# A Mamba block with a routed expert layer: steps of a round respread over two PSUM banks, activations bound in the ScalarE order, transfers taken out of a branch

## The chip, the cores and the metric

The kernel runs on one core of a Trainium2 chip. The metric is the device time of one execution in microseconds (us), as the median of several runs. The profile comes from one further execution, which has a time of its own.

## The reference

The input is a sequence of T = 4096 tokens of width D = 256, in float32. Cut to what matters:

```python
xz = x @ W_in                                   # 256 -> 2 * 512
y = depthwise_conv(xz[:, :512], conv_w, 4 taps, causal) + conv_b
convolved = silu(y)
x_dbl = convolved @ W_x                         # delta (1), B (16), C (16)
delta = softplus(x_dbl[:, :1])
h[t] = exp(delta[t] * A) * h[t-1] + delta[t] * B[t] * convolved[t, :16]
ssm_out[t] = sum(h[t] * C[t])                   # one number per token
out = ((ssm_out + convolved * D_param) * silu(xz[:, 512:])) @ W_out
x = layernorm(x + out)
expert = argmax(x @ Wr.T + br)                  # one of 8 experts per token
x = layernorm(x + W2[expert] @ relu(W1[expert] @ x + b1[expert]) + b2[expert])
```

Each expert has W1 of 1024 x 256 and W2 of 256 x 1024. Only the chosen expert of a token is computed in the kernel.

## The kernel before

**First half, by rounds.** The tokens are cut into NB = 8 tiles of TB = 512. The loop over `k` (L752) is a software pipeline. Round k projects tile k in eight steps `project(k, 0..7)` (two matmuls of 128x512 each, into a PSUM tile `pm`), and between these steps it does pieces of older tiles: of tile a = k-1 `gauge` (delta, B and C, PSUM tiles `px` and `pxo`), `look_out` (the router's raw scores, `pf`) and `scan` (`pt`); of tile b = k-2 `gate` (`py`), four `project_out` (`po`) and `choose` (the expert of each token); of tile c = k-3 `rank` (a token's place in its expert's list, `pr`), `blocks_of` (a table of blocks, `pn`), `place` (writes the lists, `pz`) and `tokens_of` (looks a block's tokens up, `pi`).

**Second half, by blocks.** A block is 128 tokens of one expert; there are at most NSB = 39, and `SURE` = 37 is the number that is always worked off outside the branch. A block has four quarters: `hidden(b, 0)`, `hidden(b, 1)` (PSUM `ph`, 16 matmul records each), `close(b, 0)`, `close(b, 1)` (PSUM `pe`). `close(b, 1)` adds the token and the bias, does the layer norm and writes the 128 rows to `out` with an indirect DMA ("the scatter", L432). `turn(b)` transposes the gathered tokens (`pg`, then a VectorE copy to `xgT`). `expert(n)` takes the next n quarters; a table `fill` says how many go between the steps of rounds 6 and 7, and after the rounds a written-out list mixes the last steps with `expert` calls. The rest of the quarters then runs alone: this stretch is called the plain tail below.

**What sets the order.** TensorE's (PE's) order is the program's order (L100). On the other engines a scheduler orders the instructions; they then run in that order, each waiting on semaphores. PSUM has eight banks: three under the tag `mm` (`pm`, `ph`), three under `o` (`py`, `po`, `pe`) and two under `tr`, which `px`, `pxo`, `pr`, `pn`, `pf`, `prx`, `pz`, `pt`, `pi` and `pg` take in turn. So each user of `tr` waits until the second last one before it has been read out.

**Transfers of the blocks.** `prefetch(b)` issues, on GpSimd's (POOL's) queue, the gather of a block's tokens (`xg`, four buffers) and of its expert's 2.2 MB of weights (`we`, three buffers), up to `AHEAD` = 2 blocks ahead and here not beyond block 36. A scatter to `out` waits for the scatter before it to land, since both write `out`.

**The branch.** When the table of the last tile is built, every engine loads the number of tokens, `total`, into a register (L267). After block 34 comes the branch for blocks 37 and 38; it holds their gathers, their weights and their scatters. Blocks 35 and 36 come behind it:

```python
    quarters = blocks(0, SURE - 2)
...
    with tc.If(held[0] > (SURE - EARLY[6]) * P, preferred_fallthrough_block=False):
        for _ in blocks(SURE, NSB):
            pass
    for _ in blocks(SURE - 2, SURE):
        pass
```

With these inputs the branch is not taken.

Of the kernel before, what the change touches and what calls it, by code (L numbers as in the profile page):

```python
# [33 lines left out]
F32 = mybir.dt.float32  # L34
# [3 lines left out]
AF = mybir.ActivationFunctionType  # L38
# [5 lines left out]
P = 128  # L44
# [3 lines left out]
TB = 512  # L48
# [31 lines left out]
def mamba_moe(  # L80
# [158 lines left out]
    def table(b0, nb, columns, rows, early):  # L239
# [110 lines left out]
        nc.scalar.copy(wout[:, :, D : D + NE], pov)  # L350


    xgs, wes, turned, hid, last, open_ = {}, {}, {}, {}, {}, {}
    current = 0

    def prefetch(b):
        for n in range(b, min(b + AHEAD, SURE - 1) + 1) if b < SURE else (b,):
            if n in index and n not in xgs:
                xgs[n] = m3.tile([P, D], F32, tag="xg", name=f"xg{n}", bufs=4)
                nc.gpsimd.indirect_dma_start(  # L360
                    out=xgs[n], out_offset=None, in_=x1d[0 : index[n][0], :],
                    in_offset=bass.IndirectOffsetOnAxis(ap=index[n][1], axis=0),
                )
            if n in weights and n not in wes:

                wes[n] = (
                    wes[SURE] if n > SURE else m3.tile([P, WROW], F32, tag="we", name=f"we{n}")
                )
                nc.gpsimd.indirect_dma_start(  # L369
                    out=wes[n][:, :], out_offset=None, in_=experts,  # L370
                    in_offset=bass.IndirectOffsetOnAxis(ap=weights[n], axis=0),
                )

    def turn(b):

        px = bank("tr", f"pg{b}", 2)
        for dc in range(DC):
            nc.tensor.transpose(
                px[:, dc * P : (dc + 1) * P], xgs[b][:, dc * P : (dc + 1) * P], ident
            )  # L380
        turned[b] = (
            turned[SURE] if b > SURE else m2.tile([P, DC * P], F32, tag="xgT", name=f"xgT{b}")
        )
        nc.vector.tensor_copy(turned[b], px[:, 0 : DC * P])

    def hidden(b, half):
# [23 lines left out]
    def close(b, half):  # L410
        xg, we = xgs[b], wes[b]
        hT = hid[b]
        if half == 0:
            open_[b] = bank("o", f"pe{b}")
        py = open_[b]
        for fc in range(half * FC // 2, (half + 1) * FC // 2):
            at = O2 + fc * D
            nc.tensor.matmul(  # L418
                py[:, 0:D], lhsT=hT[:, fc, :], rhs=we[:, at : at + D],
                start=(fc == 0), stop=(fc == FC - 1),  # L420
            )
# [10 lines left out]
        nc.gpsimd.indirect_dma_start(  # L432
            out=out, out_offset=bass.IndirectOffsetOnAxis(ap=index[b][1], axis=0),
            in_=y[:, 0, :], in_offset=None, bounds_check=T - 1, oob_is_err=False,
        )

    def blocks(*span):

        nonlocal current
        for b in range(*span):  # L440
            current = b
            prefetch(b)
            if b not in turned:
                turn(b)
            hidden(b, 0)
            yield
            hidden(b, 1)
            yield
            if b + 1 in xgs:
                turn(b + 1)  # L450
            close(b, 0)
            yield
            close(b, 1)
            yield

    quarters = blocks(0, SURE - 2)

    def expert(n=1):
        for _ in range(n):
            next(quarters)  # L460
# [3 lines left out]
    def project(i, c):  # L464

        s = st[i]
        xTb = s["xTb"]
        if c == 0:
            s["xc"] = a2.tile([P, CC, KC - 1 + TB], F32, tag="xc", name=f"xc{i}")
            s["cv"] = a3.tile([P, CC, TB], F32, tag="cv", name=f"cv{i}")  # L470
            s["sg"] = a3.tile([P, CC, TB], F32, tag="sg", name=f"sg{i}")
            if i == 0:
                nc.gpsimd.memset(s["xc"][:, :, 0 : KC - 1], 0.0)
            else:
                nc.gpsimd.tensor_copy(
                    s["xc"][:, :, 0 : KC - 1], st[i - 1]["xc"][:, :, TB : TB + KC - 1]
                )
        xc, cv, sg = s["xc"], s["cv"], s["sg"]
        pm = bank("mm", f"pm{i}_{c}")
        for dc in range(DC):  # L480
            nc.tensor.matmul(  # L481
                pm, lhsT=win[:, dc, c * P : (c + 1) * P], rhs=xTb[:, dc, :],
                start=(dc == 0), stop=(dc == DC - 1),
            )
        if c >= CC:
            nc.scalar.activation(sg[:, c - CC, :], pm, AF.Silu)  # L486
            return
        nc.scalar.copy(xc[:, c, KC - 1 :], pm)  # L488
        acc = a3.tile([P, TB], F32, tag="acc", name=f"acc{i}_{c}")
        nc.scalar.activation(  # L490
            acc, pm, AF.Identity, scale=cw[:, c, KC - 1 : KC], bias=cb[:, c : c + 1]
        )
        for k in range(KC - 1):
            nc.vector.scalar_tensor_tensor(  # L494
                acc, xc[:, c, k : k + TB], cw[:, c, k : k + 1], acc, ALU.mult, ALU.add
            )
        nc.scalar.activation(cv[:, c, :], acc, AF.Silu)  # L497

    def gauge(i):

# [305 lines left out]
    expert(2)  # L806
    gauge_out(a)
    expert()
    rank(c)
    blocks_of(c)  # L810
    expert(2)
    project_out(b, 0)
    expert()
    look_out(a)
    project_out(b, 1)
    scan(a)
    expert()
    project_out(b, 2)
    expert()
    place(c)  # L820
    project_out(b, 3)
    choose(b)
    expert(2)
    tokens_of(c)
    gate(a)
    expert(3)
    rank(b)
    expert(2)
    project_out(a, 0)
    expert()  # L830
    project_out(a, 1)
    expert()
    project_out(a, 2)
    place(b)
    project_out(a, 3)
    choose(a)
    expert(4)
    rank(a)
    blocks_of(a)
    expert(5)  # L840
    place(a)
    expert(2)
    tokens_of(a)
    for _ in quarters:
        pass

    with tc.If(held[0] > (SURE - EARLY[6]) * P, preferred_fallthrough_block=False):
        for _ in blocks(SURE, NSB):
            pass
    for _ in blocks(SURE - 2, SURE):  # L850
        pass


# [42 lines left out]
```

## Time and profile before

| | |
|---|---|
| median of 3 runs | 561.43 us (560.48 to 561.77) |
| the profiled execution, its own time | 563.69 us |
| its span in the profile | 562.0 us |
| PE busy | 508.3 us (90%) |
| VectorE (DVE) busy | 344.7 us (61%) |
| ScalarE (ACT) busy | 223.8 us (40%) |
| POOL busy | 174.7 us (31%) |
| DMA queue of POOL (gathers, weights, scatters) | 91.65 MB, 43.8% of 16 engines' span |
| weights of a block, issue to landing | 9.7 us (median of 37) |

Busy time is the time in which an engine has an instruction in work. Idle time before an instruction is put down to the event that came last before it, its releaser; `DVE oh L667` is a VectorE instruction of line 667 that writes `oh`. "PEclk" is the TensorE clock that was granted, as a share of the full one. The 1.69 us between the span and the execution's own time lie outside the span.

### The profile page before, as it was taken

What the parts mean: (1) busy time and instruction counts of PE and PEld (TensorE: products, weight loads), DVE (VectorE), ACT (ScalarE), POOL (GpSimd) and SP (SyncE); (2) the same over time, 40 slices, a digit from 0 to 9 for tenths busy, and PEclk for the clock granted to TensorE, in tenths of its full rate; (3) what the DMA queues carried; (4) which work ended last, traced back from release to release, by engine and by line L of the source; (5) the groups of instructions that cost most, each with busy time, mean ns of one, the idle gap of its engine ahead of it and who ended that gap; (6) DMA issues with size and microseconds to landing.
All of it is one profiled execution on the core that took longest, in us unless ns stands there. A gap on an engine that the chain in (4) does not pass through costs nothing. (4 is left out here: it accounts for less than half of the span.)

```text
span 562.0 us, 7926 instructions
## 1 busy us (share of the span) xinstructions
PE 508.3 (90%) x2780; PEld 385.7 (69%) x2780; DVE 344.7 (61%) x1156; ACT 223.8 (40%) x461; POOL 174.7 (31%) x191
## 2 busy tenths in 40 slices
PE   5898999898889499999789998999999999999890
PEld 2353545455354377577578787999999999999790
DVE  0656969496976684995748868545555444445531
ACT  0858768475746365564733202111111111111110
POOL 2001221233353241442333322334433343444210
PEclk9989999899979699999979999999999999999997
DMA  8201012120319404604646556989989999999800
GB/s 239 83 23 38 0 38 75 35 79 1 114 43 428 156 10 169 227 17 170 219 147 260 206 200 213 342 316 341 346 329 348 336 345 340 336 346 349 326 21 0
DMA packets 23018, 106.94 MB, mean 190 GB/s; under 512 B 4254, under 2 KB 13473, under 8 KB 18242
## 3 DMA queue, kind: packets, MB, share of 16 engines
q0 software_dynamic: 8880, 91.65, 43.8%
q1 hardware_dynamic: 11072, 12.85, 7.1%
q10 hardware_dynamic: 3026, 1.93, 1.4%
q8 instruction: 23, 0.38, 0.3%
q14 instruction: 17, 0.14, 0.1%
HBM read 98.02 MB, written 9.04 MB: 191 GB/s over the span
## 5 line engine op out<-in xcount | busy, mean ns | idle before, releaser
L396 PEld LDWEIGHTS ph<-xgT,we 128*128 128x128 f32 x1184 | 139.8, 194 | 12.0 <-ACT cv L497 4.7
L396 PE MATMUL ph<-xgT,we 128*128 128x128 f32 x1184 | 141.6, 278 | 6.7 <-ACT cv L497 4.4
L418 PE MATMUL pe<-we,hT 128*128 128x256 f32 x592 | 137.4, 384 | 4.1 <-issue 2.6
L481 PE MATMUL pm<-xTb,win 128*128 128x512 f32 x256 | 125.8, 627 | 8.2 <-DMA win<-in_W_in 5.1
L418 PEld LDWEIGHTS pe<-we,hT 128*128 128x128 f32 x592 | 110.8, 193 | 18.8 <-issue 2.7
L481 PEld LDWEIGHTS pm<-xTb,win 128*128 128x128 f32 x256 | 48.7, 200 | 60.5 <-issue 42.0
L494 DVE SCALAR_TENSOR_TENSOR acc<-xc,cw,acc 128x512 f32<-128x512 f32 x96 | 78.3, 838 | 18.8 <-ACT acc L490 18.2
L221 ACT ACTIVATE sdm<-sdm 128x1 f32<-128x1 f32 x37 | 7.5, 202 | 172.1 <-DVE sdm L220 172.0
L432 POOL DMA_INDIRECT out<-y,tidx x37 | 37.7, 1018 | 104.4 <-DVE hT L406 45.8
L406 DVE TENSOR_SCALAR hT<-ph,we 128x128 f32<-128x128 f32 x148 | 42.3, 345 | 43.9 <-PE ph L396 43.9
L616 PE MATMUL po<-wout,sg 128*128 128x264 f32 x256 | 66.4, 404 | 0.0
L369 POOL DMA_INDIRECT we<-in_experts,widx x37 | 35.6, 963 | 72.9 <-issue 24.2
L616 PEld LDWEIGHTS po<-wout,sg 128*128 128x128 f32 x256 | 47.9, 197 | 11.7 <-issue 4.8
L404 ACT ACTIVATE hT<-ph,we 128x128 f32<-128x128 f32 x148 | 42.1, 367 | 28.9 <-PE ph L396 20.3
L429 DVE TENSOR_TENSOR r<-pe,xs 128x256 f32<-128x256 f32 x37 | 15.7, 424 | 59.6 <-PE pe L418 59.6
L360 POOL DMA_INDIRECT xg<-x1d,tidx x37 | 37.3, 1007 | 31.5 <-DVE lg L657 9.3
L582 POOL TENSOR_TENSOR sg<-cv,sg 128x512 f32<-128x512 f32 x22 | 29.4, 1362 | 36.2 <-DVE cv L578 36.2
L620 DVE TENSOR_TENSOR xb<-po,xb 128x264 f32<-128x264 f32 x32 | 13.8, 431 | 34.7 <-PE po L616 34.4
L709 POOL TENSOR_SCALAR rowh<-lrow,row,code 128x256 f16<-128x256 bf16 x20 | 25.9, 1305 | 28.0 <-DVE starts L263 10.5
L486 ACT ACTIVATE sg<-pm 128x512 f32<-128x512 f32 x32 | 18.9, 595 | 34.0 <-PE pm L481 33.8
L488 ACT COPY xc<-pm 128x512 f32<-128x512 f32 x32 | 18.5, 578 | 18.9 <-PE pm L481 18.6
L578 DVE SCALAR_TENSOR_TENSOR cv<-cv,dp,py 128x512 f32<-128x512 f32 x32 | 22.9, 739 | 3.8 <-PE py L576 3.8
(154 smaller groups left out, 503.5 us busy)
## 6 DMA issues: line engine op xcount, KB each, us to landing
xb<-in_x SPq DMA_DIRECT2D x8, 512.0 KB, 3.9
x1d<-x SPq DMA_DIRECT2D x8, 512.0 KB, 4.8
xTb<-in_xT SPq DMA_DIRECT2D x7, 512.0 KB, 3.6
we<-in_experts,widx POOLq DMA_INDIRECT x37, 9.7
xg<-x1d,tidx POOLq DMA_INDIRECT x37, 5.3
out<-y,tidx POOLq DMA_INDIRECT x37, 6.6
wout<-in_W_out ACTq DMA_DIRECT2D x1, 512.0 KB, 9.2
woutT<-in_W_outT ACTq DMA_DIRECT2D x1, 512.0 KB, 4.6
```

The lines of the kernel that those rows point to most:

```text
L360: nc.gpsimd.indirect_dma_start(out=xgs[n], out_offset=None, in_=x1d[0 : index[n][0], :], in_offset=bass.IndirectOffsetOnAxis(ap=index[n][1 ...
L369: nc.gpsimd.indirect_dma_start(out=wes[n][:, :], out_offset=None, in_=experts, in_offset=bass.IndirectOffsetOnAxis(ap=weights[n], axis=0),)
L396: nc.tensor.matmul(ph[:, n * P : (n + 1) * P], lhsT=we[:, at : at + P], rhs=xgT[:, dc * P : (dc + 1) * P], start=(dc == 0), stop=(dc == DC ...
L404: nc.scalar.activation(hT[:, fc, :], ph[:, n * P : (n + 1) * P], AF.Relu, bias=bias)
L406: last[b] = nc.vector.tensor_scalar(hT[:, fc, :], ph[:, n * P : (n + 1) * P], bias, 0.0, ALU.add, ALU.max)
L418: nc.tensor.matmul(py[:, 0:D], lhsT=hT[:, fc, :], rhs=we[:, at : at + D], start=(fc == 0), stop=(fc == FC - 1),)
L432: nc.gpsimd.indirect_dma_start(out=out, out_offset=bass.IndirectOffsetOnAxis(ap=index[b][1], axis=0), in_=y[:, 0, :], in_offset=None, boun ...
L481: nc.tensor.matmul(pm, lhsT=win[:, dc, c * P : (c + 1) * P], rhs=xTb[:, dc, :], start=(dc == 0), stop=(dc == DC - 1),)
L494: nc.vector.scalar_tensor_tensor(acc, xc[:, c, k : k + TB], cw[:, c, k : k + 1], acc, ALU.mult, ALU.add)
L582: eng.tensor_tensor(sg[:, c, :], cv[:, c, :], sg[:, c, :], ALU.mult)
L616: nc.tensor.matmul(po[:, 0 : D + NE], lhsT=sg[:, c, j * P : (j + 1) * P], rhs=wout[:, c, :], start=(c == 0), stop=(c == CC - 1),)
L709: (nc.vector if i >= NB - 3 else nc.gpsimd).tensor_scalar(rowh[:, j, :], lrow, row[:, j : j + 1], code[:, i * JT + j : i * JT + j + 1], AL ...
```

## The change

- In a round, `look_out(a)` moves from step 4 to step 6; `rank(c)` from step 3 to step 4 and `blocks_of(c)` from step 3 to step 5; `place(c)` from step 5 to behind step 7; `tokens_of` of a tile moves from the end of its round to step 2 of the next. The list after the rounds is respread in the same manner, and `fill` has an eighth place; rounds 6 and 7 take 13 quarters of blocks instead of 18.
- ScalarE's Silu of a convolved chunk, `cv[:, c]`, is bound to come behind the read-out of the projection step two later; the three halo columns of the next tile (`xc`) are copied in step 4 of a round and not at the start of the next.
- All 37 sure blocks run ahead of the branch. Gathers and weights of blocks 37 and 38 are always fetched, ahead of it. `total` is loaded into the registers within block 34. The branch holds only the arithmetic of blocks 37 and 38, which goes to a tile `done` that was set to zero; their two scatters always run, behind the branch. Rows whose index lies beyond the last token are skipped by a scatter.

```diff
@@ table
-            held.extend(
-                nc.values_load_multi_w_load_instructions(
-                    total, min_val=0, max_val=nb * P, bass_reorder=False
-                )[1]
-            )
+            held.append(total)
@@ prefetch
-        for n in range(b, min(b + AHEAD, SURE - 1) + 1) if b < SURE else (b,):
+        for n in range(b, min(b + AHEAD, NSB - 1) + 1):
...
@@ close
-        y = m3.tile([P, 1, D], F32, tag="y", name=f"y{b}")
-        layernorm(m2, r, 1, y, f"m{b}")
+        if b < SURE:
+            ys[b] = m3.tile([P, 1, D], F32, tag="y", name=f"y{b}")
+        layernorm(m2, r, 1, ys[b], f"m{b}")
+        if b < SURE:
+            scatter(b)
+
+    def scatter(b):
         nc.gpsimd.indirect_dma_start(
             out=out, out_offset=bass.IndirectOffsetOnAxis(ap=index[b][1], axis=0),
-            in_=y[:, 0, :], in_offset=None, bounds_check=T - 1, oob_is_err=False,
+            in_=ys[b][:, 0, :], in_offset=None, bounds_check=T - 1, oob_is_err=False,
         )
@@ blocks
-            if b + 1 in xgs:
+            if b + 1 in xgs and b + 1 < SURE:
                 turn(b + 1)
...
-    quarters = blocks(0, SURE - 2)
+    quarters = blocks(0, SURE)
@@ project
-            else:
-                nc.gpsimd.tensor_copy(
-                    s["xc"][:, :, 0 : KC - 1], st[i - 1]["xc"][:, :, TB : TB + KC - 1]
-                )
...
-        nc.scalar.activation(cv[:, c, :], acc, AF.Silu)
+            s["acc", c] = acc
+        if ("acc", c - 2) in s:
+            with tc.issue_after(evicted.ins):
+                nc.scalar.activation(cv[:, c - 2, :], s["acc", c - 2], AF.Silu)
+        if c == CC and i + 1 < NB:
+            after = st[i + 1]["xc"] = a2.tile(
+                [P, CC, KC - 1 + TB], F32, tag="xc", name=f"xc{i + 1}"
+            )
+            nc.gpsimd.tensor_copy(after[:, :, 0 : KC - 1], xc[:, :, TB : TB + KC - 1])
@@ the rounds
-        fill = {NB - 2: (0, 1, 1, 1, 1, 2, 2), NB - 1: (1, 1, 1, 2, 1, 2, 2)}.get(k, (0,) * 7)
+        fill = {NB - 2: (0, 0, 0, 0, 0, 1, 2, 2), NB - 1: (1, 1, 1, 1, 1, 1, 1, 1)}.get(k, (0,) * 8)
...
         project(k, 2)
+        if have(c - 1):
+            tokens_of(c - 1)
...
         project(k, 3)
...
-        if have(c):
-            rank(c)
-            blocks_of(c)
...
         project(k, 4)
-        if have(a):
-            look_out(a)
+        if have(c):
+            rank(c)
...
         project(k, 5)
+        if have(c):
+            blocks_of(c)
         look(k)
...
-        if have(c):
-            place(c)
...
         project(k, 6)
         if have(a):
+            look_out(a)
             scan(a)
...
         project(k, 7)
         if have(c):
-            tokens_of(c)
+            place(c)
+        expert(fill[7])
@@ after the rounds
     for _ in quarters:
-        pass
-
-    with tc.If(held[0] > (SURE - EARLY[6]) * P, preferred_fallthrough_block=False):
+        if current == SURE - 3 and len(held) == 1:
+            held += nc.values_load_multi_w_load_instructions(
+                held[0], min_val=0, max_val=NSB * P, bass_reorder=False
+            )[1]
+
+    done = a2.tile([P, NSB - SURE, D], F32, tag="xb", name="done")
+    nc.vector.memset(done, 0.0)
+    for b in range(SURE, NSB):
+        ys[b] = done[:, b - SURE : b - SURE + 1, :]
+    with tc.If(held[1] > (SURE - EARLY[6]) * P, preferred_fallthrough_block=False):
         for _ in blocks(SURE, NSB):
             pass
-    for _ in blocks(SURE - 2, SURE):
-        pass
+    for b in range(SURE, NSB):
+        scatter(b)
```

PE's order around the first blocks, as the two programs have it (PSUM tiles by tile or block number; `pm6_2` is step 2 of round 6):

```
before  pm5_3 pxo4 pr2 pn0 po3_0 ... pm5_7 pi0 pm6_0 py4 pm6_1 px5 pg0 ph0_0 pm6_2 ...
after   pm5_3 pxo4 po3_0 pm5_4 pr2 po3_1 pm5_5 pn0 prx5 ... pm6_1 px5 pm6_2 pi0 pm6_3 pxo5
        po4_0 pm6_4 pr3 po4_1 pm6_5 prx6 po4_2 pg0 ph0_0 pm6_6 ...
before  pm7_7 pi5 py6 px7 pg5 pe4 ...
after   pm7_7 pz4 ph3_0 py6 px7 ph3_1 pg4 pe3 pi5 pxo7 pe3 ph4_0 po6_0 ph4_1 pr5 po6_1 pg5 pe4 ...
```

More of the change, by code (lines that the diff above doesn't have):

```diff
@@ L350, in router_weights @@
         nc.scalar.copy(wout[:, :, D : D + NE], pov)
-    xgs, wes, turned, hid, last, open_ = {}, {}, {}, {}, {}, {}
+    xgs, wes, turned, hid, last, open_, ys = {}, {}, {}, {}, {}, {}, {}
     current = 0
     def prefetch(b):
-        for n in range(b, min(b + AHEAD, SURE - 1) + 1) if b < SURE else (b,):
+        for n in range(b, min(b + AHEAD, NSB - 1) + 1):
             if n in index and n not in xgs:
@@ L364, in prefetch @@
             if n in weights and n not in wes:
-                wes[n] = (
-                    wes[SURE] if n > SURE else m3.tile([P, WROW], F32, tag="we", name=f"we{n}")
-                )
+                wes[n] = m3.tile([P, WROW], F32, tag="we", name=f"we{n}")
                 nc.gpsimd.indirect_dma_start(
@@ L380, in turn @@
             )
-        turned[b] = (
-            turned[SURE] if b > SURE else m2.tile([P, DC * P], F32, tag="xgT", name=f"xgT{b}")
-        )
+        turned[b] = m2.tile([P, DC * P], F32, tag="xgT", name=f"xgT{b}")
         nc.vector.tensor_copy(turned[b], px[:, 0 : DC * P])
@@ L468, in project @@
         if c == 0:
-            s["xc"] = a2.tile([P, CC, KC - 1 + TB], F32, tag="xc", name=f"xc{i}")
+            if i == 0:
+                s["xc"] = a2.tile([P, CC, KC - 1 + TB], F32, tag="xc", name="xc0")
+                nc.gpsimd.memset(s["xc"][:, :, 0 : KC - 1], 0.0)
             s["cv"] = a3.tile([P, CC, TB], F32, tag="cv", name=f"cv{i}")
             s["sg"] = a3.tile([P, CC, TB], F32, tag="sg", name=f"sg{i}")
-            if i == 0:
-                nc.gpsimd.memset(s["xc"][:, :, 0 : KC - 1], 0.0)
-            else:
-                nc.gpsimd.tensor_copy(
-                    s["xc"][:, :, 0 : KC - 1], st[i - 1]["xc"][:, :, TB : TB + KC - 1]
-                )
         xc, cv, sg = s["xc"], s["cv"], s["sg"]
@@ L485, in project @@
         if c >= CC:
[L486 to L495, printed above, removed]
-            )
-        nc.scalar.activation(cv[:, c, :], acc, AF.Silu)
+            evicted = nc.scalar.activation(sg[:, c - CC, :], pm, AF.Silu)
+        else:
+            nc.scalar.copy(xc[:, c, KC - 1 :], pm)
+            acc = a3.tile([P, TB], F32, tag="acc", name=f"acc{i}_{c}")
+            evicted = nc.scalar.activation(
+                acc, pm, AF.Identity, scale=cw[:, c, KC - 1 : KC], bias=cb[:, c : c + 1]
+            )
+            for k in range(KC - 1):
+                nc.vector.scalar_tensor_tensor(
+                    acc, xc[:, c, k : k + TB], cw[:, c, k : k + 1], acc, ALU.mult, ALU.add
+                )
[6 more added lines that the diff above has]
+                [P, CC, KC - 1 + TB], F32, tag="xc", name=f"xc{i + 1}"
+            )
+            nc.gpsimd.tensor_copy(after[:, :, 0 : KC - 1], xc[:, :, TB : TB + KC - 1])
     def gauge(i):
@@ L806, in mamba_moe @@
     expert(2)
+    tokens_of(c - 1)
     gauge_out(a)
-    expert()
-    rank(c)
-    blocks_of(c)
     expert(2)
@@ L813, in mamba_moe @@
     expert()
+    rank(c)
+    project_out(b, 1)
+    expert()
+    blocks_of(c)
+    project_out(b, 2)
+    expert()
     look_out(a)
-    project_out(b, 1)
     scan(a)
     expert()
-    project_out(b, 2)
+    project_out(b, 3)
+    choose(b)
     expert()
     place(c)
-    project_out(b, 3)
-    choose(b)
+    expert()
+    gate(a)
     expert(2)
     tokens_of(c)
-    gate(a)
-    expert(3)
+    expert(2)
     rank(b)
-    expert(2)
     project_out(a, 0)
@@ L833, in mamba_moe @@
     project_out(a, 2)
+    expert()
     place(b)
@@ L838, in mamba_moe @@
     rank(a)
+    expert(2)
     blocks_of(a)
-    expert(5)
+    expert(3)
     place(a)
-    expert(2)
+    expert(3)
     tokens_of(a)
     for _ in quarters:
-        pass
-    with tc.If(held[0] > (SURE - EARLY[6]) * P, preferred_fallthrough_block=False):
+        if current == SURE - 3 and len(held) == 1:
[7 more added lines that the diff above has]
+    with tc.If(held[1] > (SURE - EARLY[6]) * P, preferred_fallthrough_block=False):
         for _ in blocks(SURE, NSB):
             pass
-    for _ in blocks(SURE - 2, SURE):
-        pass
+    for b in range(SURE, NSB):
+        scatter(b)
 def kernel(**inputs):
```

## The prediction

> **What bounds the kernel.** I read the page first, to see which engine has work all the time, then PE's waits, then the granted clock around the longest waits, then the order of time at the two ends.
>
> ```profile
> PE 508.3 (90%) x2780; PEld 385.7 (69%) x2780; DVE 344.7 (61%) x1156; ACT 223.8 (40%) x461; POOL 174.7 (31%) x191
> PEclk9989999899979699999979999999999999999997
> ```
>
> PE is the bound: 508.3 of 562.0 us. What a change of order can win is PE's idle time, 53.7 us, and the dips of its clock.
>
> ```profile
> PE pg L378 <- DMA xg<-x1d,tidx: 5.1, 1, 5.1
> ...
> PE ph L396 <- ACT cv L497: 4.4, 1, 4.4
> PE pg L378 <- DVE cv L578: 4.2, 1, 4.2
> PE pz L723 <- POOL rowh L709: 3.9, 4, 1.0
> PE pn L249 <- ACT sr L527: 3.3, 1, 3.3
> PE pm L481 <- ACT acc L490: 3.1, 2, 2.8
> PE pe L418 <- issue: 2.6, 1, 2.6
> PE pr L679 <- DVE oh L667: 2.5, 3, 0.8
> PE ph L396 <- DVEq L847: 2.3, 1, 2.3
> PE pe L418 <- DVE hT L406: 1.5, 2, 1.1
> ```
>
> These are PE's waits (total, times, longest). None lies in the plain tail, 347.4 to 531.4 us, where PE is busy 183.99 of 184.00 us. Next, four stretches behind such waits (us, PE busy, granted clock):
>
> ```profile
> 102.00:105.00 3.00, 3.00 (x11) 0.70 0.00 0
> 156.00:160.00 4.00, 3.86 (x10) 0.50 0.00 2
> 191.00:195.00 4.00, 3.76 (x17) 0.50 0.02 4
> 283.00:286.00 3.00, 3.00 (x9) 0.50 0.06 20
> ```
>
> After a wait PE works on at a lower clock for some us; the waits cost twice. Last the timeline: a VectorE instruction beside POOL's products in round 6, and POOL's last three scatters.
>
> ```profile
> 180.52 4.89 DVE L494 SCALAR_TENSOR_TENSOR acc<-xc,cw,acc 128x512 f32<-128x512 f32 x1
> 181.13 3.72 POOL L582 TENSOR_TENSOR sg<-cv,sg 128x512 f32<-128x512 f32 x3
> ...
> 535.83 1.00 POOL L432 DMA_INDIRECT out<-y,tidx  x1 [6.93 <-issue]
> 543.71 0.98 POOL L432 DMA_INDIRECT out<-y,tidx  x1 [6.88 <-DVE y L224]
> 550.96 0.98 POOL L432 DMA_INDIRECT out<-y,tidx  x1 [6.26 <-DVE y L224]
> ```
>
> **Rounds 3 to 5: waits of the `tr` banks, -10.0 us.** `pr` waits 2.5 for the choice `oh`, `pn` 3.3 + 0.3 for the bank of `pxo`, `pz` 3.9 for `rowh`. In the new order `pr` comes one `po` and one projection step later (1.87 + 1.81 us by their starts) than a wait of 0.8; `pn` comes two steps and two `po` behind `pxo` (some 7.4 us against 3.3). From `pr` to the last `rowh` it took 12.7 us in round 4 (121.7 to 134.4); `pz` now stands about 12.7 us behind `pr`, and VectorE, which took up `pr` only 4.8 us after it, will be further along. All three go: 2.5 + 3.6 + 3.9 = 10.0. What is late next is VectorE: see below.
>
> **Round 6: the first block, -8.6 us.** `pg` of block 0 waited 4.2 and its `ph` 4.4. The token gather was issued at 177.65, 2.8 us after `pi` (174.88), and landed at about 186.2, behind three weights transfers issued from 164.7 on. Now 12.5 us of PE work lie between `pi` and `pg` (three `pm`, three `po`, `pxo`, `pr`, `prx`), against 2.8 + 8.5 = 11.3 needed; and `pg` stands 30.5 us behind `pn`, as long as the weights and the gather took from 156.1 to 186.2 (30.1). So the cover is 0.4 to 1.2 us thin. On POOL the gather is moved behind three products `sg` (3.72 us); in round 5 they ended 6.3 us behind `py`, and `pi` now comes 6.6 us behind it, so they are done. The `ph` still has to wait for its `xgT`: VectorE reads out `po` first (0.43), then copies (0.42): +0.7 us with latencies.
>
> **Drain and halo: -6.6 us.** `pg` of block 5 waited 5.1 for a gather that came 8.6 us after `pi`; now 10.3 us of work lie between (`pxo`, two `po`, three quarters of blocks, `pr`). The two `hT` waits (1.5) came from table work queued ahead of `hT` on VectorE; in the new order this work stands behind. The Silu bound behind two read-outs adds no instruction; ACT is 40% busy and the `cv` of a tile is read a round later. The halo copies (some 0.5 us on POOL) leave the start of a round, where VectorE needs them. I cost both at nothing; if `cv` came late, `px` would pay at most its 0.63 us.
>
> **Clock: -8.8 us.** Time at a clock below full, times what is missing: 3 x 0.30 + 3 x 0.27 behind 102; 3.86 x 0.5 + 3 x 0.2 behind 156; 3.76 x 0.5 + 0.5 behind 186; 3 x 0.5 + 3 x 0.25 behind 283: 1.7 + 2.5 + 2.4 + 2.2. The Trainium skill (TensorE: Matmul & The Clock Gate, What's actually happening) has half the clock after an idle window of about 3.4 us. That would let the 1.7 us behind two waits of 0.97 us stand as accident, since round 4 had the same waits at a clock of 1.00; by it the sum would be 1.7 smaller if the dip came back.
>
> **Branch and registers: -3.8 us.** PE waited 2.3 at the branch for block 34's last VectorE work; behind block 36 nothing is left for PE to wait for. Of the 2.6 us at the register load, VectorE wrote `total` only at 345.99 and PE went on at 347.39, so the load is 1.3 and stays (in block 34), 1.3 goes. The idle `turn(37)` goes: 0.2. The loads on VectorE, ACT and POOL fall into the plain tail, where each is idle half the time.
>
> **New: VectorE's lag, +2.6 us.** A round without waits is 28.1 us of PE (`py` to `py` in round 4 30.9 less 2.8), and VectorE is busy 25.5 of it. `sg` for `po` was ready 8.4 us behind `py` and gets one `acc`, one `cv` place later (9.4) while PE arrives at 9.2; `sr` for `pt` was ready 20.5 behind `py` and PE arrives at 21.4 instead of 24.9. I put 0.4 for each of rounds 3 to 7 (2.0) and 0.6 for `pg` of block 6, whose bank `pt` is read out by a scan behind table work. Bounds: 0, and 5 x 2.2 (what POOL's products cost VectorE in round 4: 1.27 for 0.18 and 1.81 for 0.74).
>
> **New: the end, +7.1 us.** Three things. First, weights of block 38 are now in flight when block 36 ends, as those of block 36 were when block 34 ended: there `y` was ready at 533.59 and the scatter went at 535.83, since the scatter before took 7.1 us to land; block 36's went after 0.28. That is +2.0. Then the scatters of 37 and 38 follow one another, each waiting for the one before to land: before the first 2.4 (535.83, nothing else in flight), before the second 2.1 (the last one of before, which moved 0.01 MB; these two write nothing), and 0.3 from landing to issue each: +5.1. What came behind the last issue (550.96 to 562.0) I keep. Lower bound 4.8 (no delay of block 36's scatter, 2.1 each), upper 16.8 (2.0 + 2 x (7.1 + 0.3), both landing as under load). I take the unloaded rows, since no weights follow block 38's. The two more weights transfers cost PE nothing: they have 13.74 us from issue to use in the tail and land in 9.7.
>
> **Sum.** -10.0 - 8.6 - 6.6 - 8.8 - 3.8 = -37.8; + 0.7 + 2.6 + 7.1 = +10.4. Together -27.4: span 534.6, the profiled execution 563.69 - 27.4 = 536.3. The median of the runs is 2.26 below that execution, so 561.43 - 27.4 = **534.0 us**.
>
> **Rivals.**
>
> *VectorE and POOL set the pace.* The 4.89 us instruction above (its like take 0.74) stood still while POOL ran three products. If each of five rounds meets the 2.2 us of round 4 and PE has no slack for it, 11.0 stand for 2.0, and a `pt` a little late costs clock: 534 + 9 + 1 = 544. The Trainium skill (SBUF — State Buffer, Who interferes with whom) has it as a lock that one instruction holds to its end. For it: 25.5 of 28.1 us. Against: `rowh` on POOL (129.4 to 134.4) left small VectorE instructions at 0.15 to 0.35.
>
> *The gathers still come late.* Cover for block 0 is 0.4 to 1.2 us. If the weights hold the gather up for as long as before, 8.6 and 2.4 of clock come back: 545; with block 5's 5.1 and 2.2 too, 552. For it: one weights transfer took 18.1 us. Against: it needs `pg` to be reached no later than before.
>
> *The change does not do what it says:* the next user of a bank waits instead, and waits and clock stay: 561.4 - 3.8 + 7.1 = 564.7. Against: `pr` and `pz` waited for data, not for banks.
>
> *Slower: weights become the bound of the plain tail.* Blocks start it with three more behind them, some 26 in all, at a DMA share of 0.91 and 338 GB/s; POOL's scatters already go 2.2 us late from block 15 on, each held by the one before. If a block takes as long as its transfers, the whole gain is gone at 27.4 / 26 = 1.05 us more than 7.25, that is at 8.3 us a block, or about 295 GB/s; at 8.5 us it ends at 566. Against: no wait of PE in 184 us, and the lag does not grow.
>
> **Chances.** Forecast 0.62 (527 to 541: no lag and the short end, 528, down to some scatter of runs; up to 2.6 + 4 more on the lag); VectorE's pace 0.15; late gathers 0.12; no effect on the waits 0.05; weights 0.05; 0.01 within 0.2% (about 1.1 us, what a measurement of this kernel tells from no change). Faster by over 0.2%: 0.62 + 0.15 + 0.12 = 0.89; slower 0.10. The range reaches to 550, which takes in VectorE's pace, the upper bound of the end (543.7) and most of the late gathers: 527 to 550.
>
> **What would show it.** Right: PE's list of waits without `pz`, `pn` and `pr`; `pg` of block 0 and of block 5 without a DMA or VectorE wait over 1 us; a clock of 1.0 from round 3 to the end of block 36; rounds of 28 to 29 us; PE working through from block 34 to 36; behind the last `y` three scatters, 2.4 us apart. Wrong: waits of PE of 1 us or more at `po` or `pt` in every round (VectorE), PE waits on `we` in the tail (weights), or an end longer than 18 us behind the last `y`.

## The result and the profile after

The changed kernel takes 529.69 us (median of 4 runs, 527.79 to 531.23), beside 561.6 us for the kernel before in the same runs: a ratio of 0.943 (95% interval 0.9392 to 0.9467). The forecast was 534.0 us, in a range from 527 to 550. The profiled execution took 530.13 us and its span is 528.4 us, 33.6 less than before; 27.4 less was forecast.

Two rows of the page of the changed kernel answer to the first two of before.

```profile
PE 499.0 (94%) x2778; PEld 381.3 (72%) x2778; DVE 345.7 (65%) x1156; ACT 220.5 (42%) x459; POOL 181.5 (34%) x197
PEclk9899999999999979999999999999999999999996
```

PE's busy time fell by 9.3 us (508.3 to 499.0) and its idle time by 24.3 (53.7 to 29.4). Before, five slices ahead of the last two had a digit below 9. Two such are left: the second (13 to 26), at the start of the kernel, and the fifteenth (185 to 198). PE's waits (total, times, longest):

```profile
PE pm L473 <- DMA win<-in_W_in: 5.1, 1, 5.1
PE pm L473 <- ACT acc L482: 2.5, 1, 2.5
PE pg L371 <- DMA xg<-x1d,tidx: 2.3, 1, 2.3
PE ph L387 <- DVE xgT L375: 2.0, 1, 2.0
PE pt L560 <- DVE sr L552: 1.2, 1, 1.2
PE py L578 <- DVE hC L571: 0.9, 1, 0.9
```

`pz`, `pn`, `pr`, the `hT` waits, the wait at the branch and `pg` of block 5 have left the list. The first two waits lie in the first 16 us of the kernel and were there before (5.1, and 2.8 as the longest of two); `pt` waits at 46 us, ahead of round 3, where 0.6 was waited before, and `py` at 51 us, as before. Below these rows stand two of 0.5: `prx` in round 5 and a `pxo` in the list after the rounds, both for VectorE. What is left of the change's own places is the first block: `pg` 2.3, `ph` 2.0. Now PE busy and granted clock by stretch (us, PE busy, then the other engines, clock behind POOL's count):

```profile
78.00:105.36 27.36, 27.36 (x112) 15.09 (x112) 23.89 (x77) 21.50 (x36) 10.17 (x9) 1.00 0.19 63
105.36:132.70 27.34, 27.34 (x112) 15.08 (x111) 24.53 (x76) 21.19 (x34) 10.10 (x9) 1.00 0.18 58
...
185.00:189.00 4.00, 3.99 (x17) 3.92 (x18) 0.47 (x2) 0.17 (x1) 2.38 (x2) 0.50 0.00 0
189.00:193.00 4.00, 4.00 (x17) 2.44 (x16) 0.00 (x0) 2.56 (x7) 0.36 (x1) 0.83 0.00 0
...
322.00:513.00 191.00, 191.00 (x1315) 179.98 (x1315) 94.01 (x319) 35.07 (x130) 75.33 (x77) 1.00 0.92 342
```

The first two rows are rounds 3 and 4, from `py` to `py`: 27.4 us each, without any idle time of PE, at full clock (round 4 of before: 30.9). The last one is the plain tail, which now runs through without a pause, branch and register load included. The two rows between show half the clock behind the first block's waits.

The end of the span is read on POOL, in the order of time:

```profile
514.65 1.01 POOL L428 DMA_INDIRECT out<-y,tidx  x1 [5.79 <-DVE r L420]
518.92 0.99 POOL L428 DMA_INDIRECT out<-y,tidx  x1 [3.26 <-DMA out<-y,tidx]
521.80 0.97 POOL L428 DMA_INDIRECT out<-done,tidx  x1 [1.90 <-DMA out<-y,tidx]
524.62 0.97 POOL L428 DMA_INDIRECT out<-done,tidx  x1 [1.85 <-issue]
```

These are the scatters of blocks 35 to 38. `y` of block 36 was ready at 516.37 and its scatter went 2.55 later, since the one of block 35 had not landed; then each link of the chain takes 2.9 and 2.8 us (2.1 to land, some 0.75 to the next issue). But from the last issue to the end of the span it is only 3.8 us, against 11.0 before. The rows of POOL's queue at the last line of the kernel say why (durations in ns: shortest, median, longest; then the starts of the first and the last in us); first before, then after:

```profile
L892 POOLq DRAIN  x3: 45/113/10372, 550.7 to 561.7; - x3
```

```profile
L906 POOLq DRAIN  x3: 45/112/2802, 524.4 to 528.1; - x3
```

One DRAIN on POOL's queue took 10.37 us before and takes 2.80 now. What this instruction waits for, the profile does not name. I had read those 11 us as a fixed tail of every execution. They are not.

### The profile page after: what moved, and what is told of

It reads as the page before. It is cut to its first block, busy times and chain, and to the rows that moved or that the text cites. A ratio compares the mean times of both kernels' runs of the same rounds, so it can differ in the third digit from the quotient of the medians.

```text
span 528.4 us, 7923 instructions
## 1 busy us (share of the span) xinstructions
PE 499.0 (94%) x2778; PEld 381.3 (72%) x2778; DVE 345.7 (65%) x1156; ACT 220.5 (42%) x459; POOL 181.5 (34%) x197
## 5 line engine op out<-in xcount | busy, mean ns | idle before, releaser
L409 PE MATMUL pe<-we,hT 128*128 128x256 f32 x592 | 135.5, 380 | 0.0
L473 PE MATMUL pm<-xTb,win 128*128 128x512 f32 x256 | 124.5, 620 | 7.5 <-DMA win<-in_W_in 5.1
L409 PEld LDWEIGHTS pe<-we,hT 128*128 128x128 f32 x592 | 109.3, 190 | 14.4 <-DVE xs L418 0.8
L486 DVE SCALAR_TENSOR_TENSOR acc<-xc,cw,acc 128x512 f32<-128x512 f32 x96 | 76.5, 822 | 11.5 <-ACT acc L482 11.0
L618 PE MATMUL po<-wout,sg 128*128 128x264 f32 x256 | 64.1, 393 | 0.0
L362 POOL DMA_INDIRECT we<-in_experts,widx x39 | 38.3, 982 | 63.9 <-DVE r L420 17.3
L618 PEld LDWEIGHTS po<-wout,sg 128*128 128x128 f32 x256 | 46.3, 190 | 9.3 <-issue 2.9
L584 POOL TENSOR_TENSOR sg<-cv,sg 128x512 f32<-128x512 f32 x22 | 31.7, 1457 | 31.5 <-DVE cv L580 19.7
L482 ACT ACTIVATE acc<-pm,cb,cw 128x512 f32<-128x512 f32 x32 | 25.1, 783 | 0.0
```

The source lines that it names most:

```text
L362: nc.gpsimd.indirect_dma_start(out=wes[n][:, :], out_offset=None, in_=experts, in_offset=bass.IndirectOffsetOnAxis(ap=weights[n], axis=0),)
L409: nc.tensor.matmul(py[:, 0:D], lhsT=hT[:, fc, :], rhs=we[:, at : at + D], start=(fc == 0), stop=(fc == FC - 1),)
L473: nc.tensor.matmul(pm, lhsT=win[:, dc, c * P : (c + 1) * P], rhs=xTb[:, dc, :], start=(dc == 0), stop=(dc == DC - 1),)
L482: evicted = nc.scalar.activation(acc, pm, AF.Identity, scale=cw[:, c, KC - 1 : KC], bias=cb[:, c : c + 1])
L486: nc.vector.scalar_tensor_tensor(acc, xc[:, c, k : k + TB], cw[:, c, k : k + 1], acc, ALU.mult, ALU.add)
L584: eng.tensor_tensor(sg[:, c, :], cv[:, c, :], sg[:, c, :], ALU.mult)
```

## The experiments

Ratios are to the kernel before, in the same runs, with 95% intervals.

| kernel | median us | ratio | POOL's longest DRAIN, us |
|---|---|---|---|
| changed kernel | 529.69 | 0.943 (0.9392 to 0.9467) | 2.80 |
| front_only | 539.09 | 0.9582 (0.9521 to 0.9643) | 10.36 |
| tail_only | 557.36 | 0.9892 (0.983 to 0.9954) | 2.80 |
| no_empty | 525.73 | 0.9342 (0.9283 to 0.9401) | 2.77 |
| later_block | 528.84 | 0.9402 (0.9341 to 0.9464) | 2.80 |
| after_again | 530.06 | 0.9432 (0.9405 to 0.9459) | 2.79 |
| unbound_silu | 530.81 | 0.9452 (0.9416 to 0.9487) | 2.80 |
| old_steps | 547.38 | 0.9759 (0.971 to 0.9809) | 2.80 |
| turn_ahead | 522.36 | 0.9299 (0.9269 to 0.9329) | 2.80 |
| turn_branch | 518.56 | 0.9207 (0.915 to 0.9264) | 2.04 |
| no_guard | 523.43 | 0.9286 (0.9232 to 0.9341) | 10.35 |
| poke | 524.64 | 0.931 (0.9262 to 0.9358) | 10.38 |
| all_in_branch | 526.52 | 0.9368 (0.9327 to 0.9409) | 9.15 |

**The two halves of the change.** `front_only` has the new order of the rounds and the bound Silu, and everything from `blocks(0, SURE - 2)` to the end as before. `tail_only` has the old order with the new end.

> The new order of the rounds and of the list behind them, and the bound Silu, with the end of the kernel before: register load at the table of the last tile, branch behind block 34 with its transfers inside, blocks 35 and 36 behind it. By the two traces PE ended block 34 at 531.4 before and at 499.9 after; 2.6 of that is PE's wait at the register load, which this kernel keeps. Theory (the two halves of the change are independent): -28.9, 532.7 us, PE idle 2.3 at the branch again, and POOL's DRAIN at the very end long again (10.4 before, 2.8 after). Rival (the end is cheaper for another reason than the branch, such as POOL being further ahead): the DRAIN is about 3 and the time about 525.

> The order of the kernel before with the end of the changed one: all 37 blocks ahead of the branch, transfers of blocks 37 and 38 ahead of it, two empty scatters behind it. Theory: the front's waits and clock dips stay as before; from the end of block 34 to the end 28.5 instead of 30.6 (-2.1) and no wait of 2.6 at the register load: -4.7, 556.9 us; POOL's DRAIN at the end about 3. Rival (the long DRAIN belongs to the last scatter of a mostly empty block, not to the kind of branch): DRAIN about 10, time about 564.

Measured: the order alone gives a ratio of 0.9582, some 23 us of 561; the end alone 0.9892, some 6 us. Together that makes 29.6, and the whole change gives 32. tail_only came as expected (557.36 for 556.9), front_only 6.4 later than its theory said (539.09 for 532.7). In front_only the waits that the new end takes away are still there, and the long DRAIN with them:

```profile
...
PE ph L396 <- DVE shift L273: 3.2, 1, 3.2
...
PE ph L396 <- DVEq L858: 2.3, 1, 2.3
```

```profile
L903 POOLq DRAIN  x3: 45/113/10363, 523.5 to 534.5; - x3
```

The first is the wait for the loads of `total`, the second the branch. The first was 2.6 before and had no dip behind it. Here it had one, a clock of 0.51 from 311 to 318:

```profile
311.79 6.71 PE L396 MATMUL ph<-xgT,we 128*128 128x128 f32 x32 [3.20 <-DVE shift L273]
```

32 such matmuls take 3.73 in the tail, so 3.0 of the 6.4 us lie here, and 0.6 in the longer wait; the rest I cannot place. So the end is a gain and not the loss that I had put it at (+7.1 against -3.8): the DRAIN pays for both added scatters.

**The two empty scatters.** `no_empty` leaves out the scatters of blocks 37 and 38, which write nothing with these inputs (with others, their rows would be missing).

```diff
-    for b in range(SURE, NSB):
-        scatter(b)
```

> The changed kernel without the two scatters of blocks 37 and 38 behind the branch (they write no row with these inputs; with others the rows of those blocks would be missing). They were issued at 521.80 and 524.62, the scatter of block 36 at 518.92. Theory A (POOL's long DRAIN of 10.4 us came from the branch with transfers inside): the DRAIN stays about 3 and the end comes 5.7 earlier: 524.0 us. Theory B (a long DRAIN follows when block 36's scatter is the last, as it was before): DRAIN about 10, and the time is 531 us, no faster.

Measured: 525.73 us, span 523.0, last scatter at 519.35, DRAIN 2.77. Two links of the chain are worth 4 to 5.5 us, and the DRAIN is short without them: an empty scatter at the end is not what shortens it.

**The steps of the rounds.** `old_steps` is the changed kernel with `rank`, `blocks_of`, `place` and `look_out` back at their old steps inside the rounds (`tokens_of`, the list after the rounds, `fill` and the end stay new). `after_again` is the changed kernel once more, in the same runs.

```diff
         project(k, 3)
+        if have(c):
+            rank(c)
+            blocks_of(c)
...
         project(k, 4)
-        if have(c):
-            rank(c)
+        if have(a):
+            look_out(a)
...
         project(k, 5)
-        if have(c):
-            blocks_of(c)
...
+        if have(c):
+            place(c)
         project(k, 6)
         if have(a):
-            look_out(a)
             scan(a)
...
         project(k, 7)
-        if have(c):
-            place(c)
```

> The changed kernel with rank, blocks_of, place and look_out at their old steps inside the rounds (3, 3, 5 and 4); tokens_of, fill, the list behind the rounds and the end stay as changed. Theory (the steps' places made the waits): pr, pz and pn wait again in rounds 3 to 5 (2.5 + 3.9 + 3.3 of PE before) with the clock dips of 102 and 156 us, 10 to 14 us slower than the changed kernel. Rival (VectorE's and ACT's new order alone had removed them): less than 4 us slower.

> The changed kernel once more, as the reference for the three beside it: about 0.943 of the kernel before (ratio so far 0.939 to 0.947), the same waits of PE and a short DRAIN at the end.

Measured: 547.38 beside 530.06, so 17.3 us hang on the place of four steps, more than the 10 to 14 expected. Between the two profiled executions (545.4 and 528.0 of span) 11.6 us are idle time of PE and 5.8 are busy time. PE's waits in old_steps, and its clock:

```profile
...
PE pr L681 <- ACT sr L529: 3.9, 1, 3.9
PE pz L725 <- POOL rowh L711: 3.8, 4, 1.0
PE pn L249 <- ACT sr L529: 3.3, 1, 3.3
...
PE pr L681 <- DVE oh L669: 2.3, 3, 0.8
```

```profile
PEclk9999999998989799999999999999999999999996
```

The `pr` (2.3), `pn` and `pz` waits return with nearly their old sizes, and dips of the clock with them. The first row shown is no such return: it is a wait in round 6 that the kernel before did not have, so part of the 17.3 us comes from the old steps beside the new ones. A row that names `sr` for a `pn` or `pr` is a wait for a PSUM bank of the tag `tr`: ScalarE's copy `sr` of the `pxo` just ahead is what frees it.

**The bound Silu.** `unbound_silu` takes the binding away and leaves the rest of the changed kernel.

```diff
-            s["acc", c] = acc
-        if ("acc", c - 2) in s:
-            with tc.issue_after(evicted.ins):
-                nc.scalar.activation(cv[:, c - 2, :], s["acc", c - 2], AF.Silu)
+            nc.scalar.activation(cv[:, c, :], acc, AF.Silu)
```

> The changed kernel with the Silu of each convolved chunk written again behind its own step, not bound behind the read-out of two steps later (the halo copies stay where the change put them). The prediction costed the bound Silu at nothing. Theory (ACT is 42% busy and PE has three mm banks): within 1 us of the changed kernel. Rival (a Silu that waits for VectorE holds up the read-outs behind it on ACT, and PE waits for a pm bank in rounds 3 to 7): PE waits on pm, 3 to 8 us slower.

Measured: 530.81 beside 530.06, spans of 528.0 in both. The binding is worth nothing that these runs can tell: without it the waits of `pm` (3.2 for 2.7) and `ph` (3.1 for 2.3) are a little longer, and the span is the same.

**The first block.** Why its gather was still late is read in the timeline of the changed kernel, round 6:

```profile
167.34 0.51 PE L304 MATMUL pi<-pick,lists 128*128 128x5 f32 x4
...
172.11 2.73 DVE L486 SCALAR_TENSOR_TENSOR acc<-xc,cw,acc 128x512 f32<-128x512 f32 x4
...
174.76 0.15 DVE L309 TENSOR_SCALAR half<-pi 128x5 f32<-128x5 f32 x1
...
175.92 1.31 POOL L356 DMA_INDIRECT xg<-x1d,tidx  x1 [7.51 <-DVE tidx L311]
...
182.60 0.41 PE L371 MATMUL pg<-ident,xg 128*128 128x128 f32 x2 [2.29 <-DMA xg<-x1d,tidx]
...
185.01 3.78 PE L387 MATMUL ph<-xgT,we 128*128 128x128 f32 x16 [2.00 <-DVE xgT L375]
```

`pi` was multiplied at 167.34, but VectorE read it out only at 174.76: one `cv` and one `sg` of `gate`, seven `acc` of the convolution (the last four in the second row) and small ones of the choice of experts came first in its order. So the gather went 8.6 us behind `pi`, where I had put the 2.8 of before. That ate all of the new cover, and `ph` ran at half clock (3.78 us for 16 matmuls; 32 took 3.73 in the tail). Two kernels place this block elsewhere. `later_block` only moves one quarter: its `fill` for round 6 is (0, 0, 0, 0, 0, 0, 2, 3). `turn_ahead` has the same `fill`, and puts the transposes of block 0 behind `scan` in step 6:

```diff
         if have(a):
             look_out(a)
             scan(a)
+        if k == NB - 2:
+            turn(0)
```

> The changed kernel with the first quarter of block 0 one step later in round 6 (fill 0,0,0,0,0,0,2,3 instead of 0,0,0,0,0,1,2,2). PE waited 2.3 for the token gather and 2.0 for its transposed copy there, and the clock was at half behind it (some 2.7). Theory (the gather lands 2.3 too late, and VectorE is busy with the lists of rank just then): both waits and the dip go, -5 to -7: 523 to 525 us. Rival (VectorE is the late one at any place in round 6): the gather's 2.3 goes, a wait of 2 for xgT stays with its dip: 527 us; or the later start costs cover in the drain and nothing is won, 529.7.

> The changed kernel with the first block's transpose split off: turn(0) stands in round 6 behind look_out and scan, one project_out ahead of its hidden quarters (fill 0,0,0,0,0,0,2,3). With the later start alone PE still waited 3.6 for xgT. Theory (VectorE reads out PSUM tiles in program order; once its copy stands ahead of the last po and PE has 1.9 us of other work, the wait shrinks): PE's wait for xgT under 1 us, no dip of the clock there, 4 to 7 us faster than the changed kernel. Rival (VectorE is 3.6 us behind at any place of round 6): the wait moves with it and the time stays within 2 us.

Measured: later_block took 528.84 us where 523 to 525 was expected: the `pg` wait goes, but `ph` waits 3.6 instead of 2.0 for its `xgT`, so little is won. turn_ahead took 522.36, or 7.7 us less than after_again. Its row for `ph`, and its clock:

```profile
PE ph L387 <- DVE xgT L375: 0.6, 1, 0.6
```

```profile
PEclk9999999999999999999999999999999999999995
```

No dip is left. The `pg` now stands ahead of a `po` of 1.95 us instead of right before its `ph`, so that VectorE's copy runs beside PE's work. The Trainium skill (TensorE: Matmul & The Clock Gate, What's actually happening) has half the clock after an idle window of about 3.4 us. The rows agree in kind: 2.3 + 2.0 us idle, with 0.41 of work between them, were followed by a clock of 0.50 to 0.83 until 193, and a single wait of 0.6 by none. Not all of the 7.7 us are the edit's: at the start, which the edit does not touch, the profiled execution of after_again has a clock of 0.66 from 15 to 20, some 1.7 us, and that of turn_ahead 1.00. This dip comes and goes between kernels with the same start (no_guard lacks it, poke has it).

**The end.** `turn_branch` is turn_ahead with the two last scatters in the branch, behind the arithmetic of their blocks:

```diff
         for _ in blocks(SURE, NSB):
             pass
-    for b in range(SURE, NSB):
-        scatter(b)
+        for b in range(SURE, NSB):
+            scatter(b)
```

> The version with the transpose ahead (522.4 us, 0.9299 of the kernel before) with the two scatters of blocks 37 and 38 put back into the branch; gathers and weights stay ahead of it and all 37 blocks run ahead of it. Theory A (any transfer of POOL inside the branch brings the long DRAIN, as in the kernel before: 11.0 us from the last issue to the end, against 3.8): the two links of 2.9 go and 7.2 come, 524 us. Theory B (the long DRAIN came with blocks 35 and 36 standing behind the branch): the DRAIN stays about 3 and the time is 516.7 us, a version faster than any so far.

Measured: 518.56 us, the fastest of all, 1.9 over what theory B said. Two chain links are gone, and the DRAIN is short:

```profile
L908 POOLq DRAIN  x3: 45/113/2043, 512.3 to 515.2; - x3
```

`no_guard` is turn_ahead with blocks 37 and 38, the register load and the branch left out altogether (with these inputs the blocks are empty; with others their rows would be missing). It asks whether transfers still in flight or the branch matter for the DRAIN:

```diff
-        for n in range(b, min(b + AHEAD, NSB - 1) + 1):
+        for n in range(b, min(b + AHEAD, SURE - 1) + 1):
...
-    with tc.If(held[1] > (SURE - EARLY[6]) * P, preferred_fallthrough_block=False):
-        for _ in blocks(SURE, NSB):
-            pass
-    for b in range(SURE, NSB):
-        scatter(b)
```

> The version with the transpose ahead, without blocks 37 and 38 altogether: no branch, no register load, no gathers, weights or scatters for them (with these inputs they hold no token; with others their rows would be missing). It measures what the guard at the end costs. From the last y to the end it took 12.0 us in the changed kernel and 11.3 in the one before. Theory: without weights of block 38 in flight the scatter of block 36 goes 0.3 behind its y, and 3.8 later the kernel ends: 4.1 instead of 12.0, 514.5 us. Rival (the DRAIN is long whenever POOL stands idle before the last scatter): 11.3, 521.7 us.

Measured: 523.43 us. PE's last matmul ends as in turn_branch (507.0 and 506.9 us) and the last scatter goes 0.28 us behind `y`, but the DRAIN is long again, and the kernel that does less than turn_branch is 5 us slower:

```profile
509.52 0.97 POOL L428 DMA_INDIRECT out<-y,tidx  x1 [6.05 <-DVE y L224]
```

```profile
L895 POOLq DRAIN  x3: 45/102/10353, 509.3 to 520.2; - x3
```

In all kernels with a long DRAIN the last scatter came behind some 6 us of idle time on POOL, in turn_ahead, turn_branch and no_empty behind 1.9 to 4.7. `poke` tests that: it is no_guard with a copy of 128 x 1 on POOL just ahead of the last scatter.

> The version without blocks 37 and 38 (DRAIN of POOL at the end 10.35 us, 11 us from the last issue to the end, 523.4 us, 0.9286 of the kernel before), with one POOL copy of 128x1 added in block 36, which waits for VectorE's r and so runs about 2 us ahead of the last scatter. In the three kernels with a long DRAIN (10.35 to 10.37) POOL had done nothing for 6.1 to 6.3 us ahead of its last scatter, and a VectorE event released it; in those with a short one (2.0 to 2.8) it had stood idle for 1.9 to 4.7 us, and a landing DMA released it. Theory (the idle time decides): the DRAIN is under 3 us, -7.5, 516 us (0.915). Rival (weights or other transfers in flight within the last 10 us decide, or the branch just ahead of the end): the DRAIN stays 10.35 and the time 523.4.

```profile
510.36 0.19 POOL L423 COPY awake<-r 128x1 f32<-128x1 f32 x1 [4.10 <-DVE r L420]
512.32 0.99 POOL L431 DMA_INDIRECT out<-y,tidx  x1 [1.77 <-DVE y L224]
```

```profile
L898 POOLq DRAIN  x3: 45/102/10375, 512.1 to 523.0; - x3
```

Measured: 524.64 us. That theory falls: 1.77 us of idle time, and the same DRAIN. Of the theories that I had, two were left: the branch directly ahead of the end, and the transfers. `all_in_branch` is turn_branch with the old rule of `prefetch`, so that the branch stands ahead of the end but 37 gathers and 37 weights transfers run instead of 39 (the others stand in the branch, where block 38 shares the buffers of block 37, as in the kernel before):

```diff
-        for n in range(b, min(b + AHEAD, NSB - 1) + 1):
+        for n in range(b, min(b + AHEAD, SURE - 1) + 1) if b < SURE else (b,):
```

> turn_branch with the old rule of prefetch: the gathers and weights of blocks 37 and 38 stand in the branch, beside their scatters, so 37 gathers and 37 weights transfers run instead of 39; all 37 sure blocks still stand ahead of the branch, and nothing but the branch stands between the last scatter and the end. Both theories have the last scatter at 0.3 us behind y of block 36, some 509.4 us, as in no_guard, since no weights are in flight then (turn_branch: 511.78). They part on POOL's DRAIN at the end, 10.4 us in before, front_only, no_guard and poke, 2.0 to 2.8 in the rest. Theory A, the branch ahead of the end makes it short: DRAIN about 2.0, 3.7 us from the last scatter to the end as in turn_branch, span 513.2, median about 516.3, the fastest of all. Theory B, the two further pairs of transfers make it short (all four with the long DRAIN ran 37, all others 39): DRAIN about 10.4, 10.9 us from the last scatter to the end as in no_guard, span 520.4, median about 523.4.

```profile
511.41 0.97 POOL L432 DMA_INDIRECT out<-y,tidx  x1 [6.06 <-DVEq L867]
```

```profile
L912 POOLq DRAIN  x3: 45/107/9147, 514.1 to 523.8; - x3
```

Measured: 526.52 us, span 524.1. The DRAIN is long: a branch ahead of the end does not make it short. The theory of the transfers holds in sign; the end came even later than it said, 12.7 us behind the last scatter, because the untaken branch costs POOL one more instruction of 2.42 us there (0.37 in turn_branch) before its DRAIN begins. So all five kernels with 37 pairs of gathers and weights have a long DRAIN, and all nine with 39 a short one; in the two that differ in little else, turn_branch and all_in_branch, the span is 8.6 us shorter with two more pairs, 7.1 of it by the DRAIN and 2.05 by the branch's instruction; some 0.5 goes back, most of it because the last scatter of all_in_branch went 0.37 earlier.

One more thing goes with the DRAIN in all fourteen kernels, and I did not test it. In the five with a long DRAIN POOL's DMA queue had moved nothing for 5.0 to 5.2 us when the last scatter was issued, since the scatter before it had landed some 5 us earlier; in the nine with a short one it was 1.1 to 1.2 us, since the last scatter waited for the one before. The copy in poke gave POOL work, but not its DMA queue.

## Why the prediction was right, and where it was not

The time lay in the range and the likeliest case was the one that came. Going by its steps:

- **Rounds 3 to 5, -10.0:** right in the waits, and too small in what they cost. The three kinds of wait are gone, and they return in old_steps. A wait's own row did not hold its whole price: in round 4 of before the matmuls of `pz` with their two waits of 0.97 stretched from 131.91 to the next `pm` at 134.72, 2.81 us; now the same eight take from 130.40 to 130.84.
- **VectorE's lag, +2.6:** hardly came. Rounds 3 and 4 last 27.4 us where I had 28.1 + 0.4, and PE idles in neither; what VectorE costs from round 3 on, beside the first block, is the `prx` wait of 0.5 in round 5 and the `pxo` wait of 0.5 after the rounds, so 1.0. The rival "VectorE and POOL set the pace" falls with it: VectorE is busy up to 24.5 of 27.3 us, but outside the first block late by little that PE meets.
- **First block, -8.6 + 0.7:** the mis-sized term. 4.3 us of waits stayed where I left 0.7, since I took the 2.8 us from `pi` to the gather from the old order, while in the new one the read-out of `pi` stood on VectorE behind nine long instructions (0.68 to 0.74 us each). I had counted what PE does between `pi` and `pg`, and not what VectorE does ahead of `half`. The cover of "0.4 to 1.2 us" was -2.3. Part of the rival of late gathers was therefore real.
- **Clock, -8.8:** the dips gave only 6.1. Before they cost the 8.8 and 1.7 more at 34 to 40 us (a clock of 0.72), which I had not counted. Now 1.7 are lost at 15 to 21 (0.72 again) and, in round 6, where I had 2.4 go, 3.99 x 0.50 + 4.00 x 0.17 = 2.7 still. PE's busy time fell by 9.3 all the same, beside 9.0 forecast (8.8 and `turn(37)`): some 3 us of it went at full clock, a part in `pz`, whose busy rows fell from 5.6 to 4.9. So the -8.8 was met by luck.
- **Drain and halo, -6.6:** right: no `pg` wait of block 5, no `hT` wait. That the Silu and the halo cost nothing was right too, for the Silu by unbound_silu; the halo alone was not tried.
- **Branch and registers, -3.8:** right in kind, and 1.3 too small. The load takes 0.49 us on PE's queue in the tail and shows in no wait.
- **The end, +7.1:** the step that failed is that I kept what came behind the last issue. The two pieces that I sized were near: block 36's scatter 2.55 us behind its `y` (0.28 + 2.0 forecast), the links 2.9 and 2.8 (2.4 and 2.4, with 0.3 for an issue that took 0.75). But behind the last issue 3.8 us follow instead of 11.0. From `y` of block 36 to the end it took 11.3 us before and takes 12.0 now: +0.7 for my +7.1.
- **Weights as the bound of the tail:** no. PE works 191.00 of 191.00 us there at a DMA share of 0.92.

Added up: up to its last matmul PE idled 25.0 us less (40.2 to 15.2, its idle time less the 13.5 and 14.2 us behind that matmul), where these terms had 25.5, and its busy time fell by 9.3, for 9.0. Behind that 0.7 was added, for 7.1. So nearly the whole 6.2 us between forecast and span are the end. That the first two sums came so near is in part luck: in the idle time the 3.6 us that the first block gave back were made up by the lag (1.6 less) and the registers (1.3), in the busy time its 2.7 by work at full clock that I had not counted.

## What to carry to other kernels

When a step is moved on the bound engine, count again from the producer's side: the distance that matters is from the moment at which the reading engine gets to it in its own queue, and that queue was reordered by the same change. A wait costs its idle time, often what it does to the clock behind it, and some stretching of the work around it: in old_steps 11.6 us of idle time were worth 17.3 us. And the time behind the last issue is not a constant until two kernels with different ends have shown it.

## What the runs showed of the hardware that I had not expected

- **POOL's DRAIN at the end has two lengths.** It took 10.35 to 10.38 us in before, front_only, no_guard and poke and 9.15 in all_in_branch, all with 37 gathers and 37 weights transfers, and 2.04 to 2.80 us in the nine with 39, whose last weights were issued late. All of the rows written had landed 2.1 us after the last issue in the long case of before as well. Three things go with it in all fourteen: the number of indirect DMAs (111 against 115 or 117), how recent the last large one is (issued 22.4 to 26.0 us ahead of the last scatter where the DRAIN is long, 11.1 to 16.9 where it is short), and how long POOL's DMA queue had been empty ahead of the last scatter (5.0 to 5.2 us against 1.1 to 1.2). Which one decides stays open: no kernel here parts them. Idle time on POOL just ahead of the scatter does not decide it (poke), nor does a branch ahead of the end (short in turn_branch, long in all_in_branch, and long without one in no_guard).
- **An empty scatter costs nearly as much as a full one.** The scatters of blocks 37 and 38 wrote nothing and landed 2.1 us after their issue; the full ones of blocks 34 and 35 of before, with no weights beside them, took 2.4, and the one of block 36, which wrote a few rows, 2.1. With 0.75 us to the next issue, a chain of scatters on one tensor goes at 2.8 to 2.9 us a link.
- **A branch that is not taken but holds DMAs of POOL costs POOL 0.37 to 2.42 us** for one semaphore instruction on its other side; the long one was seen where the transfers of two blocks stood in the branch (2.42 in all_in_branch, 2.38 in before), the short one where only scatters did (turn_branch). The changed kernel, whose branch holds none, has no such instruction.
